# Transfers of the preparation begun by ScalarE, rows kept six tiles ahead, state stored at every second piece

## Chip, cores and metric

The kernel runs on one core of one Trainium2 chip. The metric is the device time of one execution in microseconds (us), the median of several runs.

## What is computed

The reference takes x of 2 × 2048 tokens with 256 features and does two sublayers, each with a LayerNorm before it and one after it, and a residual. The first is attention with one head of 128 and rotary positions. The second is a mixture of experts that is run twice over the same state z:

```python
for _ in range(LOOPS):                       # LOOPS = 2
    z_norm = _rmsnorm(z, norm_w)
    logits = z_norm @ router_w               # 8 experts
    scores = softmax(logits)
    topk_vals, topk_idx = top_k(scores, 2)   # then normalised to sum 1
    mixed = 0
    for e in range(8):
        mixed += cw[:, e] * _swiglu(z_norm, w1[e], w3[e], w2[e])
    z = z + mixed                            # silu(x @ w1) * (x @ w3) @ w2, F = 512
```

The result is x1 + LayerNorm(z), where x1 is what the attention sublayer left.

## The kernel before

Everything is float32. The first 427 us are the attention, with its normalisation, projections and output; the weights of the experts are loaded to SBUF beside it and stay there. The change doesn't touch that part. The rest, about 850 us, is the mixture of experts, and it is one loop over 142 tiles: 71 for each pass over z. A tile is 128 rows, each row a (token, expert) pair; all rows of a tile belong to one expert. Rows that two groups of tokens bring are tiled apart: group 0 holds 18 of the 32 blocks of 128 tokens, group 1 holds 14, so that the routing of one group can be worked out while the tiles of the other are computed.

**One tile, from row to row.** GpSimd gathers the 128 rows of z from DRAM by an indirect transfer (xg<-zd, L948, `gather`). SyncE writes the rows of two tiles at once to DRAM in order (xs<-xg, L961, `keep`) and reads them back in four strided transfers (xb<-xs, L970, `load`), so that VectorE can turn them into 128-column blocks (xT<-xb, L257, `turned`). TensorE multiplies with w1 and w3 (p<-wall,xT, L993, `hidden`), ScalarE takes Silu (a<-p, L1002), VectorE multiplies the halves (g<-a,p, L1007, `gate`). The hidden rows go the same way: SyncE stores them in DRAM (gd<-g, L1012), reads two tiles back in four transfers (gb<-gd, L1019, `hidden_back`), VectorE turns them (gT<-gb, L257, `turn_hidden`), TensorE multiplies with w2 (py<-wall,gT, L1035, `mix`). ScalarE scales the rows (y<-py,rms, L1048, `give`), and GpSimd scatters them by an indirect transfer into a buffer in DRAM (given<-y,to, L1049) that holds both experts' rows of a token side by side.

**The order.** The kernel is a Python program that writes instructions in the order in which each engine will run them. `slot(m, ...)` (L1550) writes one step of the tile loop. It does, in this order: `hidden_back` of tiles m−3 and m−2 if m is odd, `gate` of m−1, `turn_hidden` of m−4, `give` of m−6, `fetch_rows(m)`, `turned` of m+2, then half of the preparation work, `hidden` of m, `mix` of m−5, and the other half of the preparation. In `fetch_rows` a pair's xb is loaded up to AHEAD = 4 tiles ahead, its xs is written up to AHEAD + 1 = 5 tiles ahead, and rows are gathered up to GATHER = 7 tiles ahead. Below, P(m) is the start of hidden(m) on TensorE.

**The preparation.** `advance` (L1543) takes pieces from a generator between the steps of the tile loop, each with a cost, until a credit for half a slot is used up (mostly SLOT/2 = 8). `plan` (L1574) says which generator runs from which slot on:

- from slot 0: the routing of group 1 for the first pass (`b0.before`);
- from slot 21: `a1.fetch(0, 24)` loads z of group 0 from DRAM (9 transfers z<-zd, L291), when the routing for pass two approaches;
- from about slot 42: `a1.before`. It first runs `logits`: for each block of two tiles load the rows that were given (given<-given, L308, 528 KB, two blocks ahead), multiply by the gains on ScalarE and add on VectorE (`add_first`, L329), add the second expert's rows on GpSimd (`add_second`), take the sum of squares on ScalarE. Then `route` and `lists` work out which token goes where, and at each of their first 9 pieces `store(i)` (L433) stores one block of z to DRAM (zd<-z, 264 KB), from where the tiles of pass two gather;
- from slots 68 and 78 on: the same for group 1 (`b1.fetch`, `b1.before`), 7 blocks;
- from slot 100 on: `a1.fetch(1)` loads z of group 0 again for the end; then `a1.finish` adds what pass two gave and does the last LayerNorm and the residual (given loads, x<-x1d L788, out<-z L783/L787), and `b1.ready` loads z and x1 of group 1 ahead;
- after the loop: `b1.last` finishes group 1.

All these direct transfers, those of the tile loop and those of the preparation, are begun by SyncE before the change, but for four of `last`. GpSimd begins the indirect ones.

Of the kernel before, what the change touches and what calls it, by code (L numbers as in the profile page):

```python
# [29 lines left out]
def attn_moe_kernel(  # L30
# [16 lines left out]
    nc = tc.nc  # L47

    ctx.enter_context(tc.manual_schedule())
    B, S, D = x.shape  # L50
# [29 lines left out]
    ob = out.rearrange("b s d -> (b s) d").rearrange("(n t p) d -> n p t d", t=2, p=P)  # L80
# [10 lines left out]
    x1d = [  # L91
        dram.tile([P, 2, D], F32, name=f"x1d{i}", tag=f"x1d{i}") for i in range(T // 2)
    ]
# [169 lines left out]

    SLOT, HALF = 16, 8
    STEP = 4
    sent = [[] for _ in range(LOOPS)]

    class Turn:
# [18 lines left out]
        def load(self):  # L287

            i = self.loaded
            if 2 * i < self.n:  # L290
                nc.sync.dma_start(  # L291
                    out=self.z[:, 2 * i : 2 * i + 2, :D],
                    in_=zrows(self.of_loop, self.t0 // 2 + i)[:, :, :D],
                )
                self.loaded += 1
# [89 lines left out]
        def logits(self):  # L385

            n = self.n
            last = self.loop - 1
            nc.vector.tensor_copy(self.z[:, :, D:Z], raw[:, self.ts, :])
            y = {i: self.load_given(last, i, nc.sync) for i in range(2)}  # L390
            yield SLOT
            ms = rpool.tile([P, NM], F32, tag="fl_sd", name="ms")[:, :n]
            rms = rpool.tile([P, NM], F32, tag="fl_sh", name="rms")[:, :n]
            lg = self.lg.rearrange("p e t -> p t e")
            done, part = 0, None

            for i in range(n // 2 + 4):
                if i + 2 < n // 2:
                    y[i + 2] = self.load_given(last, i + 2, nc.sync)
                if part is not None:  # L400
                    w = part.stop - part.start
                    nc.vector.tensor_tensor(
                        lg[:, part, :],
                        self.z[:, part, D:Z],
                        rms[:, part].rearrange("p (t o) -> p t o", o=1).to_broadcast([P, w, E]),
                        ALU.mult,
                    )

                    nc.vector.tensor_copy(self.z[:, part, D], rms[:, part])
                    part = None  # L410
                if 0 <= i - 3 < n // 2 and ((i - 3) % 3 == 2 or i - 3 == n // 2 - 1):
                    part = slice(done, 2 * (i - 2))
                    done = part.stop
                    w = part.stop - part.start
                    nc.vector.tensor_scalar(
                        ms[:, part], rms[:, part], 1.0 / D, RMS_EPS, ALU.mult, ALU.add
                    )
                    nc.gpsimd.tensor_tensor(rms[:, part], ms[:, part], neg_half[:, :w], ALU.pow)
                if 0 <= i - 2 < n // 2:
                    for t in range(2 * i - 4, 2 * i - 2):  # L420
                        sq = rpool.tile([P, D], F32, tag="sq", name="sq")
                        nc.scalar.activation(
                            sq, self.z[:, t, :D], AF.Square, accum_out=rms[:, t : t + 1]
                        )
                if 0 <= i - 1 < n // 2:
                    self.add_second(i - 1, y.pop(i - 1))
                if i < n // 2:
                    self.add_first(last, i, y[i])
                yield 10 if i < n // 2 else 6
            assert part is None and not y  # L430

        def store(self, i):
            nc.sync.dma_start(  # L433
                out=zrows(self.loop, self.t0 // 2 + i), in_=self.z[:, 2 * i : 2 * i + 2, :R]
            )

# [193 lines left out]
        def lists(self, pool, tag, keep):  # L630
# [12 lines left out]
            for h in range(parts + (3 if keep else 2)):  # L643
# [3 lines left out]
                if 0 <= i < parts:  # L647
# [12 lines left out]
                    if not keep:  # L660
                        yield STEP
                        if i == 0:
# [89 lines left out]
        def before(self, pool, tag, keep=True):  # L752
            self.lg = rpool.tile([P, E, NM], F32, tag="lg", name="lg")[:, :, : self.n]
            if self.loop == 0:
                yield from self.first_logits()
            else:
                yield from self.logits()

            for i, cost in enumerate(
                itertools.chain(self.route(pool, tag), self.lists(pool, tag, keep))  # L760
            ):
                if self.loop > 0 and i < self.n // 2:
                    self.store(i)
                yield cost

        def out_(self, i, z, x1, pool=False):

            mv, rstd = ln_stats(z, 2)
            yield
            nb = ln_bias(mv, rstd, 2)  # L770
            to = self.z[:, 2 * i : 2 * i + 2, :D]
            for t in range(2):
                nc.scalar.activation(
                    to[:, t, :],
                    z[:, t, :],
                    AF.Identity,
                    bias=nb[:, t : t + 1],
                    scale=rstd[:, t : t + 1],
                )
            yield  # L780
            (nc.gpsimd if pool else nc.vector).tensor_tensor(to, to, x1, ALU.add)
            yield
            nc.sync.dma_start(out=ob[self.t0 // 2 + i], in_=to)  # L783

        def load_x1(self, i, x1=None):
            if x1 is None:
                x1 = fp.tile([P, 2, D], F32, tag="x1", name="x1", bufs=3)  # L787
            nc.sync.dma_start(out=x1, in_=x1d[self.t0 // 2 + i])  # L788
            return x1

        def fetch(self, loop, cost):
# [6 lines left out]
        def finish(self):  # L798

            n = self.n // 2  # L800
            y, x1, ends = {}, {}, []
            for h in range(2 * n + 9):
                for end in list(ends):
                    if next(end, True):
                        ends.remove(end)
                i, odd = divmod(h - 7, 2)
                if not odd and 0 <= i < n:
                    ends.append(self.out_(i, self.z[:, 2 * i : 2 * i + 2, :D], x1.pop(i)))
                    next(ends[-1])
                i, odd = divmod(h - 5, 2)  # L810
                if not odd and 0 <= i < n:
                    self.add_second(i, y.pop(i))
                    x1[i] = self.load_x1(i)
                i, odd = divmod(h - 4, 2)
                if not odd and 0 <= i < n:
                    self.add_first(self.loop, i, y[i])
                i, odd = divmod(h, 2)
                if not odd and i < n:
                    y[i] = self.load_given(self.loop, i, nc.sync)
                yield 7  # L820
            assert not ends

# [34 lines left out]
        def last(self):  # L857


            n = self.n // 2  # L860
            sums, y = [], []
# [30 lines left out]
                    second = y[i][t][:, 1, :]  # L892
                    nc.scalar.mul(second, second, self.gain(self.loop, i, 1, t))

            ends = [self.out_(i, sums[i], self.x1[i], i % 2 == 1) for i in range(n)]
            weigh(0)
            weigh(1)
            for i in range(n + 3):
# [21 lines left out]

    A = ND * F
    AHEAD = 4
    GATHER = 7
    TURN = 2
    BACK = 4
    LAG = 5
# [137 lines left out]
    NJ = len(jobs)  # L1064
# [10 lines left out]
    def fetch_rows(m, rest=()):  # L1075


        nonlocal gathered, kept, loaded

        def load():  # L1080
            nonlocal loaded
            if loaded < kept:
                one, other = pair(loaded)
                one.load(other)
                loaded += 1 if other is None else 2

        def keep():
            nonlocal kept
            one, other = pair(kept)
            n = 1 if other is None else 2  # L1090
            if gathered >= kept + n:
                one.keep(other)
                kept += n

        def gather():
            nonlocal gathered
            held = sum(jobs[i].i % 2 == 0 for i in range(loaded, gathered))
            if jobs[gathered].turn.to is not None and (jobs[gathered].i % 2 or held < 2):
                jobs[gathered].gather()
                gathered += 1  # L1100

        if loaded <= min(m + AHEAD, NJ - 1):
            load()
        if kept <= min(m + AHEAD + 1, NJ - 1):
            keep()
        for _ in range(2):
            if gathered <= min(m + GATHER, NJ - 1):
                gather()
        if loaded <= min(m + TURN + 1, NJ - 1):
            while jobs[loaded].turn.to is None or jobs[min(loaded + 1, NJ - 1)].turn.to is None:  # L1110
                next(rest)
            while loaded <= min(m + TURN + 1, NJ - 1):
                gather()
                keep()
                load()
# [531 lines left out]
```

## Time and profile before

| what | value |
|---|---|
| median of 3 runs | 1275.72 us (1273.36 to 1276.16) |
| the profiled execution | 1276.36 us |
| its span, first to last instruction | 1274.6 us |
| mean granted TensorE clock in it | 0.978 |
| TensorE matmul busy | 1168.7 us (92%) |
| VectorE busy | 673.5 us (53%) |
| GpSimd busy | 519.6 us (41%) |
| ScalarE busy | 424.4 us (33%) |
| transfers on SyncE's queue (q1) | 181.85 MB, 53.5% of the 16 DMA engines' span |
| transfers on GpSimd's queue (q0) | 37.61 MB, 10.6% |
| transfers on ScalarE's queue (q10) | 3.16 MB, 0.7% |

The profile names an operation by the program's names, what it writes and what it reads (`xb<-xs`), with the line. PE is TensorE's matmul, DVE is VectorE, ACT is ScalarE, POOL is GpSimd, SP is SyncE. "SPq" is SyncE's queue: issuing a transfer isn't counted as busy, but takes the queue's time, and a line "SPq L970 <- DMA xs<-xg" is time in which it stood before a transfer of L970 until xs had landed. The chain that ended last has TensorE for 27%, transfers for 23% (xs<-xg alone 9%), issue for 16%, SyncE's queue for 13% and VectorE for 11%. In the page's row of DMA shares the tile loop has 0.6 to 0.9 of the 16 DMA engines busy in most slices, so landings depend on what else is under way.

The stages of the tile loop, from the start of hidden(0) at 427.3 us, are, with what runs beside: to about 528 the routing of group 1; to 690 the first pass, from about 550 on with the loads of z; to 800 `a1.before`; to 850 the loads for group 1; to 956 `b1.before`; to 1131 the second pass with its loads for the end; to 1215 `a1.finish` and `b1.ready`; then the last tiles and `b1.last`.

### The profile page before, as it was taken

To read this page: it belongs to the slowest core of one execution; us is meant where nothing else is said; L and a number is where in the kernel's file an instruction comes from. 1 tells how busy PE (TensorE), PEld (TensorE's weight loads), DVE (VectorE), ACT (ScalarE), POOL (GpSimd) and SP (SyncE) were. 2 spreads that over 40 slices of the span, in tenths; PEclk is the share of its full clock that TensorE was granted. 3 is DMA by queue.
4 is the path that set the end of the run, shared out by engine and by line. 5 is a ranking of instruction groups with operands and counts; after the bars stand their busy time and mean duration, and the time that the engine had idled before them with its cause. 6 is when DMAs were issued, how large, how long until landed. Compare 5 with 4: busy or idle time off the path is not lost.

```text
span 1274.6 us, 16856 instructions
## 1 busy us (share of the span) xinstructions
PE 1168.7 (92%) x4230; PEld 719.6 (56%) x4230; DVE 673.5 (53%) x1809; ACT 424.4 (33%) x945; POOL 519.6 (41%) x870
## 2 busy tenths in 40 slices
PE   6989999999989799999999886999899999998895
PEld 3546777766666355555555444555455555554563
DVE  4646676767895457332331676334683333367224
ACT  3444343445645221221221631224312222234124
POOL 3541434341123433443442752445534444466523
PEclk9999999999999899999999987999899999999998
DMA  4124465611112577777767896899967798899955
GB/s 133 50 44 97 116 155 119 157 51 33 43 34 69 151 201 202 205 210 215 209 197 222 267 215 165 217 245 272 242 189 207 216 249 216 239 274 282 259 170 181
DMA packets 273099, 223.69 MB, mean 175 GB/s; under 512 B 112240, under 2 KB 226288, under 8 KB 273008
## 3 DMA queue, kind: packets, MB, share of 16 engines
q1 hardware_dynamic: 256640, 181.85, 53.5%
q0 software_dynamic: 13632, 37.61, 10.6%
q10 hardware_dynamic: 2736, 3.16, 0.7%
q8 instruction: 40, 0.66, 0.2%
q14 instruction: 51, 0.42, 0.1%
HBM read 130.90 MB, written 91.62 MB: 175 GB/s over the span
## 4 chain that ended last, share of the span: by engine, by line
PE 27%; DMA 23%; issue 16%; SPq 13%; DVE 11%; POOL 7%; ACT 2%; DVEq 0%; ACTq 0%; POOLq 0%
DMA xs<-xg 9%; PE sc L1357 7%; PE po L1404 6%; SPq L970 6%; PE p L993 5%; SPq L1019 5%; DMA gd<-g 4%; DMA gb<-gd 4%; PE tp_p L1391 4%; POOL xg L948 3%; PE py L1035 3%; DMA given<-given 2%; DMA xg<-zd,token 1%; PE py L1441 1%; POOL given L1049 1%
## 5 line engine op out<-in xcount | busy, mean ns | idle before, releaser
L993 PE MATMUL p<-wall,xT 128*128 x1136 | 521.2, 603 | 14.8 <-DVE xT L257 8.3
L993 PEld LDWEIGHTS p<-wall,xT 128*128 128x128 f32 x1136 | 218.1, 194 | 237.0 <-issue 223.8
L1035 PE MATMUL py<-wall,gT 128*128 x1136 | 275.3, 386 | 23.6 <-DVE gT L257 22.8
L1035 PEld LDWEIGHTS py<-wall,gT 128*128 128x128 f32 x1136 | 215.6, 191 | 120.5 <-issue 76.4
L1049 POOL DMA_INDIRECT given<-y,to x142 | 141.7, 998 | 346.9 <-ACT y L1048 321.3
L1007 DVE TENSOR_TENSOR g<-a,p 128x512 f32<-128x512 f32 x142 | 96.7, 681 | 196.4 <-issue 155.3
L257 DVE STREAM_TRANSPOSE gT<-gb 128x512 f32<-128x512 f32 x142 | 100.0, 705 | 177.8 <-DMA gb<-gd 177.8
L948 POOL DMA_INDIRECT xg<-zd,token x142 | 141.7, 998 | 89.5 <-DMA xs<-xg 66.9
L1048 ACT ACTIVATE y<-py,rms 128x264 f32<-128x264 f32 (+1 forms) x142 | 67.4, 474 | 322.2 <-PE py L1035 313.8
L1002 ACT ACTIVATE a<-p,rms 128x512 f32<-128x512 f32 x142 | 97.2, 685 | 189.8 <-PE p L993 145.7
L1357 PE MATMUL sc<-qkT 128*128 128x512 f32 x256 | 130.9, 597 | 2.0 <-ACT pr L1376 1.2
L1404 PE MATMUL po<-pt,v 128*128 128x256 f32 x512 | 127.3, 382 | 0.4 <-ACT y L1444 0.4
L1404 PEld LDWEIGHTS po<-pt,v 128*128 128x128 f32 x512 | 97.2, 191 | 51.8 <-issue 40.5
L1376 ACT ACTIVATE pr<-sc,nm 128x512 f32<-128x512 f32 x128 | 88.5, 694 | 89.1 <-DVE nm L1368 89.1
L1364 DVE TENSOR_REDUCE m<-sc 128x1 f32<-128x512 f32 x128 | 87.6, 686 | 45.4 <-PE sc L1357 44.2
L1391 PE MATMUL tp_p<-ident,pr 128*128 128x128 f32 x512 | 80.4, 276 | 10.6 <-ACT pr L1376 9.7
L1391 PEld LDWEIGHTS tp_p<-ident,pr 128*128 128x128 f32 x512 | 63.7, 143 | 40.4 <-ACT pr L1376 14.7
L185 POOL TENSOR_TENSOR rds<-rs_v,neg_half 128x2 f32<-128x2 f32 (+1 forms) x24 | 20.4, 849 | 153.7 <-DVE rs_v L184 153.1
L1395 ACT COPY pt<-tp_p 128x512 f32<-128x512 f32 x88 | 51.4, 584 | 62.2 <-PE tp_p L1391 61.4
L257 DVE STREAM_TRANSPOSE xT<-xb 128x256 f32<-128x256 f32 x142 | 57.1, 404 | 6.4 <-DMA zd<-y 4.6
L236 POOL TENSOR_SCALAR wall<-wall,nwp 128x1024 f32<-128x1024 f32 x16 | 45.6, 2850 | 10.8 <-DMA wall<-in_L_ffn_w 10.8
L1214 PE MATMUL pm<-wqkvT,hT 128*128 128x392 f32 x128 | 46.3, 505 | 0.0
(249 smaller groups left out, 978.4 us busy)
## 6 DMA issues: line engine op xcount, KB each, us to landing
gd<-g SPq DMA_DIRECT2D x142, 256.0 KB
gb<-gd SPq DMA_DIRECT2D x284, 128.0 KB
xs<-xg SPq DMA_DIRECT2D x70, 257.0 KB
xb<-xs SPq DMA_DIRECT2D x280, 64.0 KB
wall<-in_L_ffn_w SPq DMA_DIRECT2D x96, 128.0 KB
given<-given SPq DMA_DIRECT2D x16, 528.0 KB
z<-zd SPq DMA_DIRECT2D x32, 256.0 KB
given<-given SPq DMA_DIRECT2D x11, 512.0 KB
```

The lines of the kernel that those rows point to most:

```text
L257: nc.vector.transpose(out=dst.rearrange("p c (a t) -> p a c t", t=32), in_=src.rearrange("p (a c d) -> p a c d", a=4, c=n),)
L948: i = nc.gpsimd.indirect_dma_start(out=self.xg[:, k, :], out_offset=None, in_=zd[self.loop][: (SPLIT if self.i < WHOLE else T) * P, :], in ...
L993: nc.tensor.matmul(ps, lhsT=self.xT[:, c, :], rhs=wall[:, bass.ds(self.e, 1), o : o + F].rearrange("p o f -> p (o f)"), start=(c == 0), st ...
L1002: nc.scalar.activation(self.a, p1, AF.Silu, scale=self.rms)
L1007: nc.vector.tensor_tensor(g, self.a, self.p3, ALU.mult)
L1035: nc.tensor.matmul(py[:, :w], lhsT=self.gT[:, f, :], rhs=wall[:, bass.ds(self.e, 1), o : o + w].rearrange("p o d -> p (o d)"), start=(f == 0),
L1049: i = nc.gpsimd.indirect_dma_start(out=given[self.loop], out_offset=bass.IndirectOffsetOnAxis(ap=self.row(self.turn.to), axis=0), in_=y, i ...
L1357: nc.tensor.matmul(sc[u], lhsT=qkT[b][:, 0, qi * P : (qi + 1) * P], rhs=qkT[b][:, 1, c * KC : (c + 1) * KC], start=True, stop=True,)
L1364: nc.vector.tensor_reduce(nms[t][:, c : c + 1], sc[u], AX.X, ALU.max)
L1376: nc.scalar.activation(prs[u], sc.pop(u), AF.Exp, bias=nms[t], scale=SCALE, accum_out=s4s[t][:, c : c + 1],)
L1391: nc.tensor.transpose(tp[:, j, i, :], pr[:, k : k + P], ident)
L1404: nc.tensor.matmul(pos[p], lhsT=vn[p * QG // NT][:, 2 * g + j, :HD], rhs=pt[:, j, :], start=(g == 0 and j == 0), stop=(g == NS - 1 and j = ...
```

## The change

Five edits come together. A name `bulk` stands for ScalarE's queue, and the preparation's transfers are begun by it: the loads of z, of given (in `logits` and `finish`), of x1, the stores of z, and the stores of the result in `finish` (`last` keeps SyncE's). That is about 100 transfers. `logits` yields HALF once before its first loads. `store` comes at every second piece of `route` and `lists` instead of each. xs is written up to KEEP = 6 tiles ahead instead of 5 (AHEAD itself stays 4). Rows are gathered up to 8 tiles ahead instead of 7.

```diff
     SLOT, HALF = 16, 8
     STEP = 4
+
+    bulk = nc.scalar
...
-                nc.sync.dma_start(
+                bulk.dma_start(
                     out=self.z[:, 2 * i : 2 * i + 2, :D],
                     in_=zrows(self.of_loop, self.t0 // 2 + i)[:, :, :D],
...
-            y = {i: self.load_given(last, i, nc.sync) for i in range(2)}
+            yield HALF
+            y = {i: self.load_given(last, i, bulk) for i in range(2)}
             yield SLOT
...
-                    y[i + 2] = self.load_given(last, i + 2, nc.sync)
+                    y[i + 2] = self.load_given(last, i + 2, bulk)
...
         def store(self, i):
-            nc.sync.dma_start(
+            bulk.dma_start(
                 out=zrows(self.loop, self.t0 // 2 + i), in_=self.z[:, 2 * i : 2 * i + 2, :R]
...
-                if self.loop > 0 and i < self.n // 2:
-                    self.store(i)
+                j, odd = divmod(i, 2)
+                if self.loop > 0 and not odd and j < self.n // 2:
+                    self.store(j)
                 yield cost
...
-            nc.sync.dma_start(out=ob[self.t0 // 2 + i], in_=to)
+            engine.dma_start(out=ob[self.t0 // 2 + i], in_=to)
...
-            nc.sync.dma_start(out=x1, in_=x1d[self.t0 // 2 + i])
+            bulk.dma_start(out=x1, in_=x1d[self.t0 // 2 + i])
...
-                    y[i] = self.load_given(self.loop, i, nc.sync)
+                    y[i] = self.load_given(self.loop, i, bulk)
...
     AHEAD = 4
-    GATHER = 7
+    KEEP = 6
+    GATHER = 8
...
-        if kept <= min(m + AHEAD + 1, NJ - 1):
+        if kept <= min(m + KEEP, NJ - 1):
             keep()
```

More of the change, by code (lines that the diff above doesn't have):

```diff
@@ L761, in before, with out_ @@
             ):
-                if self.loop > 0 and i < self.n // 2:
-                    self.store(i)
+                j, odd = divmod(i, 2)
+                if self.loop > 0 and not odd and j < self.n // 2:
+                    self.store(j)
                 yield cost
-        def out_(self, i, z, x1, pool=False):
+        def out_(self, i, z, x1, engine, pool=False):
             mv, rstd = ln_stats(z, 2)
@@ L807, in finish @@
                 if not odd and 0 <= i < n:
-                    ends.append(self.out_(i, self.z[:, 2 * i : 2 * i + 2, :D], x1.pop(i)))
+                    ends.append(self.out_(i, self.z[:, 2 * i : 2 * i + 2, :D], x1.pop(i), bulk))
                     next(ends[-1])
@@ L893, in weigh @@
                     nc.scalar.mul(second, second, self.gain(self.loop, i, 1, t))
-            ends = [self.out_(i, sums[i], self.x1[i], i % 2 == 1) for i in range(n)]
+            ends = [self.out_(i, sums[i], self.x1[i], nc.sync, i % 2 == 1) for i in range(n)]
             weigh(0)
```

## The prediction

> **What bounds the kernel now.** I read the shares first, then TensorE by stage, then SyncE's waits, then timelines. TensorE is busy 1168.7 of 1274.6 us, but that is an average. The windows view for the first expert matmul alone (line L993, 8 records a tile; columns: window, length, matmul busy and records, weight loads, clock, DMA share, GB/s) shows where it isn't the limit:
>
> ```profile
> 427.30:528.00 100.70, 73.59 (x160) 30.63 (x160) 0.98 0.68 190
> 528.00:690.00 162.00, 107.91 (x241) 45.81 (x242) 1.00 0.75 208
> 690.00:800.00 110.00, 57.59 (x119) 23.66 (x119) 0.89 0.84 218
> 800.00:850.00 50.00, 33.83 (x76) 14.25 (x75) 1.00 0.92 235
> 850.00:956.00 106.00, 67.38 (x144) 27.72 (x143) 0.97 0.87 234
> 956.00:1131.00 175.00, 122.27 (x272) 51.48 (x271) 1.00 0.85 228
> 1131.00:1215.00 84.00, 48.24 (x105) 20.31 (x106) 0.98 0.96 271
> ```
>
> Where TensorE never waits a tile takes 5.21 us in the first loop (3.43 for L993, 1.78 for L1035) and 5.16 in the second. Records/8 times that, against the length: 956–1131 is full (34 tiles, 175.4 of 175). 690–800 loses 110−14.9×5.21 = 32.5 us, 850–956 loses 106−18×5.16 = 13.1, 1131–1215 loses 84−13.1×5.16 = 16.3, 528–690 about 5, and tiles 12 to 19 of the first window 3.6 by their starts. That is 70 us, and all the change can win. Who is late there? SyncE's own waits (us in total, times, longest):
>
> ```profile
> SPq L970 <- DMA xs<-xg: 103.3, 33, 5.7
> SPq L1012 <- DVE g L1007: 71.0, 39, 7.0
> SPq L1019 <- DMA gd<-g: 40.5, 24, 4.6
> SPq L970 <- DMA z<-zd: 1.6, 3, 0.7
> SPq L970 <- DMA given<-given: 1.5, 2, 1.1
> SPq L970 <- DMA zd<-z: 1.3, 2, 1.0
> ```
>
> SyncE begins every transfer of the tile loop in program order and stands at each wait with all later ones behind it. The last three lines matter more than their size: xb (L970) uses nothing of z, given or zd. In the kernel as built, SyncE and ScalarE draw all transfers' completion counters from one set of eight, in program order, and a transfer waits until its counter's previous user has landed.
>
> How an in-order SyncE costs time, in the timelines of ScalarE, SyncE and TensorE at the start of 690–800:
>
> ```profile
> 686.68 0.69 ACT L1002 ACTIVATE a<-p,rms 128x512 f32<-128x512 f32 x1 [1.24 <-PE p L993]
> 701.50 0.92 ACT L329 ACTIVATE given<-given,gains 128x264 f32<-128x264 f32 x2 [14.13 <-DMA given<-given]
> ```
> ```profile
> 683.62 0.43 SPq L1012 DMA_DIRECT2D gd<-g  x1
> 688.44 2.94 SPq L970 DMA_DIRECT2D xb<-xs  x4
> ...
> 694.52 1.48 SPq L308 DMA_DIRECT2D given<-given  x3
> ```
> ```profile
> 703.85 3.52 PE L1035 MATMUL py<-wall,gT 128*128 x8 [5.06 <-DVE gT L257]
> ```
>
> SyncE stood 4.8 us for xs, began given only at 694.5, given took 7.0 us to 701.5, and ScalarE stood at its multiplication for 14.13 us with y and Silu of the tile loop behind it. The start of hidden(52) came 11.97 us after hidden(51)'s, 6.8 too late. Later steps of this stage: 57→58 12.54, 60→61 16.25, 61→62 8.24.
>
> **The change part by part.** *Moving about 100 transfers from SyncE to ScalarE.* Each costs SyncE 0.5–0.6 us (z 0.60, zd 0.57, given 0.5), so some 55 us of SyncE work leave, and ScalarE gets them at 0.39–0.59 each (its few own). ScalarE is busy 35.3 of 110 us in 690–800, and its idle time ahead of y (322 us in all) hides most; without that cover each is half a microsecond ahead of a Silu. Ten loads and nine stores there, a third exposed and waiting a little for counters themselves: I take 4 us, bounds 0 and 10.
>
> The Trainium skill (page "DMA: Bandwidth & Descriptors", section "Issuing engines are not separate DMA queues") speaks against the part: starting transfers on several engines only saves the sequencer's issue time, since all run on the same DMA engines. By that rule the gain is at most the exposed part of 55 us, near nothing, because landings don't get shorter (DMA share 0.84–0.96). The rows say that the loss is order, not issue time: the 8 us by which given began late and the 6.8 us after it. I take the rows: that stall goes. But the same order turns round:
>
> *The counters now tie two engines together.* In the changed kernel as built, some 80 SyncE transfers wait for a ScalarE transfer to land, many for one that ScalarE begins one or two tiles later. Before, both stood in SyncE's own order, and the earlier had mostly landed. Price: ScalarE begins a bulk transfer 0.6 us (after y) or 4.8 us (after Silu) after the start P(n) of hidden(n) in its tile; it is released at R, that plus the landing. Landings (issue to landing, medians of the trace): z 4.5, given 6.9, zd 5.7–7.6, x1 6.2. Where xb of tile A waits, the rest of xb (1.2), xs (0.4), gd's landing, three gb issues (1.4), gb's landing and the transposition (0.7) follow, due 3.5 us into tile A+4 for its mix: P(A+4) ≥ R + gd + gb + 0.2. Where xs waits, R − 1.0 + gd + gb. Free is 10.3 to 10.4 us from P(A+2) to P(A+4). gd lands in 3.1–3.3 in quiet stretches, 5.8–6.3 in crowded ones, gb in 4.0 and 4.8. Stage by stage:
>
> 956–1131 (z for the last finish, tiles 101–109): xb of 101, 103, 105, 107 wait for the z load two tiles on. R = P(A+2)+0.6+4.5 = 5.1; 5.1+3.3+4.0+0.2 = 12.6 against 10.3: +2.3 a pair, four pairs, and gb of 101 +1.3: **+10.5**, in a stage that loses nothing now. 800–850 (z of the second group): the same for 69 and 71: **+4**.
>
> 850–956: xs of 75 waits for given of 77's second half: 4.8+6.9−1.0+3.9+4.4 = 19.0, +8.7; xs of 77 for given of 79: 0.6+6.9+7.3 = 14.8, +4.5; xs of 85 for zd of 87: 13.6, +3.3; small ones 0.4. That is 17, and I leave 3 of the old 13.1: **+7**.
>
> 690–800: the stalls of 51/52 and most of the three that followed go, 3 of 32.5 stay. New: gb of 49 waits for given of 50: its gT is there at 5.2+0.6+7.0+1.4+4.0+0.7 = 18.9 after P(49), due at 13.9: +5; xb of 50 and 52 +1 each; gd of 59 behind zd of 59's second half +3; ScalarE 4. 14+3 = 17 left of 32.5: **−15**.
>
> 1131–1215: xb of 121, 131, 133 and xs of 135 wait for x1 or z two tiles on, 14.9 each by quiet landings, 17–18 by crowded ones: 16 to 29 us in all against 16.3 now; I take 22: **+6**.
>
> *Rows six ahead, gathers eight.* As built, xs stands one tile earlier in SyncE's order, so xb finds it landed. In 528–690 SyncE's round is xs landing 5.0 + issues 5.6 = 10.6 a pair against TensorE's 10.42; the wait goes, and so do the 5 us there, and about 2 in tiles 12–19. z loads of tiles 22–32 give 3.5 back by ties one tile long: **−1** and **−2**.
>
> *Stores at every second piece, HALF before the first given.* Nine stores of 264 KB now begin one piece apart; the chain of waits has them in this stage, at 742–766:
>
> ```profile
> 744.29 6.65 DMA gb<-gd
> 751.00 9.51 DMA zd<-z
> 760.57 0.55 SPq L433
> ```
>
> Spacing them takes crowding from gd and gb (medians 5.8 and 5 there, 3.1 and 4.0 quiet); counted in the −15. The last store comes nine pieces later, and gathers wait for it and for the lists, still unfinished then: 0, at most +5. HALF moves one start by half a tile: 0.
>
> Sum: −2 −1 −15 +4 +7 +10.5 +6 = +9.5. The profiled execution took 1276.4 us (span 1274.6), 0.6 above the median 1275.7: 1285.9 on its scale, **1285** on the median's.
>
> **The rivals.** *A, the forecast (0.46)*: ties cost about what their sums say, the stage that was full loses 10, 690–800 wins 15: 1278 to 1300.
> *B, faster (0.26)*: SyncE reaches the tied transfers late anyway. A tie is free if released before P(A+2)+2.8 (10.3−7.5); z would have to land 2.2 us after its start rather than 4.5, or SyncE's program would have to run a tile ahead now that its own 55 us and its 103.3 us of xs waits are gone, so that tied transfers have a tile's slack. Then 690–800 wins 22, 850–956 and 1131–1215 8 each, the early stages 4: 1276−42 = 1234; with half of the ties paid, 1250. For it: the xs wait is the largest in SyncE's list. Against it: the sums already spend the slack that there is (in 956–1131 gd begins 4.4 us after its hidden, the mix comes 29.3 after).
> *C, much slower (0.20)*: ScalarE's transfers wait in turn for counters of SyncE's tied ones, and Silu and y stand behind them, as behind given at 687–701. With the long landings of the trace (given 9.9, zd 10.8, gd 7.8–10.5) the same sums give +36: 1312.
> *D, no change (0.08)*: wins and ties cancel, 1276.
>
> **How the numbers follow.** What a measurement of this kernel can tell from no change is about 0.2%, 2.6 us. B gives faster 0.26, D same 0.08, A and C slower 0.66. The range leaves out the far ends of B and C: 1248 to 1308. A's own is 1278 to 1300.
>
> **What would show it.** Right: records of L993 in a 956–1131-like stretch pace at over 5.4 us a tile for tiles 101–110; SyncE's waits at L970 and L1012 ended by z, given, zd, x1 grow from 1–2 us to tens; the xs line falls from 103 to under 40; ScalarE's 14 us stop ahead of L329 is gone. Wrong: tiles 101–110 still at 5.16 (B), or ScalarE's queue waiting ahead of its transfers for over 1 us at many places (C). If gd and gb land in 3–4 us in 690–800, B's −22 there holds even with ties.

## The result, and the profile after

The changed kernel is slower: 1317.95 us median (1315.82 to 1321.79), against 1274.54 us for the kernel before, run beside it. The ratio is 1.035 with a 95% interval of 1.031 to 1.039. The forecast was 1285 us and its range ended at 1308. The profiled execution has a span of 1318.0 us, 43.4 more than before.

Below, the loss of a stage is counted by tiles, not by fixed times, since the stages shift: the time from the start of hidden of its first tile to that of its end tile, less 5.21 us (first pass) or 5.16 us (second) a tile. "Beside" names the preparation that runs there.

| tiles | beside | before, us | after, us | difference | forecast |
|---|---|---|---|---|---|
| 12–20 | routing of group 1, first pass | 3.6 | 1.4 | −2.2 | −2 |
| 20–50 | z loads | 4.5 | 0.1 | −4.4 | −1 |
| 50–66 | a1.before | 34.1 | 25.5 | −8.6 | −15 |
| 66–74 | z loads of group 1 | 0.2 | 0.7 | +0.5 | +4 |
| 74–92 | b1.before | 13.9 | 32.4 | +18.5 | +7 |
| 92–118 | z loads for the end | 0.0 | 10.2 | +10.2 | +10.5 |
| 118–136 | a1.finish, b1.ready | 14.3 | 38.8 | +24.5 | +6 |

The rest is 4.5 us behind the start of the last hidden (54.2 after 49.7), about 1 at the start and −0.8 in tiles 136–141. The sum is 43.4 but for rounding.

SyncE's waits in the kernel after (us in total, times, longest), in answer to those of before:

```profile
SPq L1024 <- DMA gd<-g: 119.9, 39, 5.1
SPq L1017 <- DVE g L1012: 78.2, 30, 7.4
SPq L975 <- DMA given<-given: 32.7, 7, 8.4
SPq L1024 <- DMA z<-zd: 21.1, 5, 10.1
SPq L975 <- DMA z<-zd: 18.7, 8, 5.4
SPq L975 <- DMA xs<-xg: 10.7, 5, 2.9
```

The 103.3 us for xs are 10.7, as the row edit promised. In their place SyncE stands for transfers that xb (L975) and gb (L1024) use nothing of. All its waits for given, z, zd, x1 and out come to 127 us, against 10.9 before. The traces show the link: SyncE's and ScalarE's transfers report their landing on the same eight semaphores, GpSimd's on eight others. The wait for gd's landing ahead of gb has tripled (40.5 before), but that is no sign of loss: in e1 and e2 below, which are faster than the kernel before, it is 115.0 and 122.5 us.

In the stage that was full, the timelines of SyncE and ScalarE show one such tie:

```profile
1044.48 0.42 SPq L1017 DMA_DIRECT2D gd<-g  x1
1044.95 5.36 SPq L975 DMA_DIRECT2D xb<-xs  x4
1050.42 0.54 SPq L966 DMA_DIRECT2D xs<-xg  x1
```
```profile
1045.84 0.47 ACT L1053 ACTIVATE y<-py,rms 128x256 f32<-128x256 f32 x1 [2.75 <-PE py L1040]
1045.84 0.53 ACTq L293 DMA_DIRECT2D z<-zd  x1
```

Four xb issues take 2.6 us when nothing holds them, and 5.36 here: the third waited until 1049.09 for the z load that ScalarE began at 1045.84 and that landed at 1049.08. In tiles 100–112 the stage lost 10.1 us where 10.5 was forecast, and SyncE stood 9.7 us for z loads there. The sum agrees better than its parts: the forecast had 2.3 us at each of four pairs of tiles, and the trace has 6.6 us at one step (105 to 106) and 0.5 to 1.9 at three others.

Around 1149 us, in tiles 118–136, the same views show what the price list did not have:

```profile
1149.02 0.60 ACT L777 ACTIVATE z<-z,ln_nb,ln_rstd 128x256 f32<-128x256 f32 x1 [12.00 <-DVE ln_nb L206]
1149.08 0.53 ACTq L310 DMA_DIRECT2D given<-given  x1
1149.52 0.59 ACT L777 ACTIVATE z<-z,ln_nb,ln_rstd 128x256 f32<-128x256 f32 x1
1149.65 0.73 ACTq L792 DMA_DIRECT2D x<-x1d  x1
```
```profile
1118.41 10.86 SPq L975 DMA_DIRECT2D xb<-xs  x4
...
1135.46 1.80 SPq L1024 DMA_DIRECT2D gb<-gd  x4
...
1145.56 1.80 SPq L1024 DMA_DIRECT2D gb<-gd  x4
1147.40 0.45 SPq L1017 DMA_DIRECT2D gd<-g  x1
1148.07 8.69 SPq L975 DMA_DIRECT2D xb<-xs  x4
1157.17 0.34 SPq L966 DMA_DIRECT2D xs<-xg  x1
```

In the second of these views SyncE, at 1118.41, issued one xb and then stood 8.4 us until a given load that ScalarE had begun at 1117.66 had landed (1127.38). VectorE then stood 4.1 us for these xb and later 4.2 us for the gb that SyncE began at 1135.46. ScalarE stood 12.00 us for the bias of a LayerNorm (ln_nb) that VectorE had not got to; for 2.2 us of it VectorE stood for GpSimd. Behind ScalarE's wait lay given and x1, and SyncE's last two xb issues came at 1155.49 and 1156.13, the latter as x1, begun at 1149.65, landed (1156.12). So a tie had its part in making late the engine that begins the transfers of the next ties: a ring through engines that all work in order. The prediction let ScalarE begin a transfer 0.6 or 4.8 us after P(n); here it was later by the length of ScalarE's own wait.

### The profile page after: what moved, and what is told of

Its sections match the earlier page's. It is cut to its first block, busy times and chain, and to the rows that moved or that the text cites. A ratio compares the mean times of both kernels' runs of the same rounds, so it can differ in the third digit from the quotient of the medians.

```text
span 1318.0 us, 16792 instructions
## 1 busy us (share of the span) xinstructions
PE 1183.7 (90%) x4230; PEld 728.8 (55%) x4230; DVE 672.7 (51%) x1809; ACT 424.9 (32%) x945; POOL 521.2 (40%) x870
## 4 chain that ended last, share of the span: by engine, by line
PE 49%; DMA 16%; DVE 12%; issue 10%; POOL 7%; SPq 3%; ACT 2%; ACTq 0%; POOLq 0%; DVEq 0%
PE p L998 20%; PE py L1040 10%; PE sc L1362 6%; PE po L1409 5%; PE tp_p L1396 3%; DMA gd<-g 3%; DMA gb<-gd 3%; DMA given<-given 3%; POOL xg L953 2%; POOL given L1054 2%; DMA xs<-xg 2%; SPq L975 2%; PE py L1446 1%; DMA z<-zd 1%; DVE m L1369 1%
## 5 line engine op out<-in xcount | busy, mean ns | idle before, releaser
L998 PE MATMUL p<-wall,xT 128*128 x1136 | 525.0, 606 | 13.9 <-DMA xb<-xs 8.7
L998 PEld LDWEIGHTS p<-wall,xT 128*128 128x128 f32 x1136 | 220.3, 196 | 238.3 <-issue 224.3
L1040 PE MATMUL py<-wall,gT 128*128 x1136 | 283.9, 395 | 51.2 <-DVE gT L257 36.9
L1040 PEld LDWEIGHTS py<-wall,gT 128*128 128x128 f32 x1136 | 220.6, 196 | 151.3 <-issue 104.5
L236 POOL TENSOR_SCALAR wall<-wall,nwp 128x1024 f32<-128x1024 f32 x16 | 45.6, 2852 | 10.9 <-DMA wall<-in_L_ffn_w 10.9
L1362 PEld LDWEIGHTS sc<-qkT 128*128 128x128 f32 x256 | 41.9, 193 | 9.1 <-issue 3.4
```

The costliest lines, as they stand in the source:

```text
L998: nc.tensor.matmul(ps, lhsT=self.xT[:, c, :], rhs=wall[:, bass.ds(self.e, 1), o : o + F].rearrange("p o f -> p (o f)"), start=(c == 0), st ...
L1040: nc.tensor.matmul(py[:, :w], lhsT=self.gT[:, f, :], rhs=wall[:, bass.ds(self.e, 1), o : o + w].rearrange("p o d -> p (o d)"), start=(f == 0),
L1362: nc.tensor.matmul(sc[u], lhsT=qkT[b][:, 0, qi * P : (qi + 1) * P], rhs=qkT[b][:, 1, c * KC : (c + 1) * KC], start=True, stop=True,)
```

## The experiments

Theory T is the forecast's: the loss is the tie of SyncE's transfers to ScalarE's through counters that both draw from one set. Its rivals were that the row edit or the later stores hurt, that two queues crowd the DMA engines, and that ScalarE's own order holds its transfers. Ratios are to the kernel before, run beside each. There the kernel before took 1287 to 1290 us, not the 1274.5 of the main result, and there is no trace of it from there. So ratios are the measure of what an edit costs; losses by tiles, which come from one trace each, can be compared with those of the kernel before or the changed one only with a doubt of up to 12 to 16 us in all. Traces of different runs whose code is the same up to tile 66 differ by up to 3 us in 50–66.

### The parts alone

**e1**: the row edit alone.

```diff
-    GATHER = 7
+    KEEP = 6
+    GATHER = 8
...
-        if kept <= min(m + AHEAD + 1, NJ - 1):
+        if kept <= min(m + KEEP, NJ - 1):
```

> Only the row edit: xs written up to six tiles ahead and rows gathered up to eight ahead; all direct transfers stay on SyncE, stores at every piece. Theory T (the loss of the whole change is the tie of SyncE's transfers to ScalarE's through shared completion counters): this part is a gain by itself, the 4.4 us of tiles 20-50 and about 2 of tiles 12-20 go, some of the 34, 14 and 14 us of the three preparation stages too: 1262 to 1270 us. Rival R1 (deeper rows crowd the DMA engines, so gd and gb land later): 1276 to 1290.

Measured: 0.991 (0.988 to 0.994). Right in size, and it disposes of R1 for the whole kernel. But the stages surprised: 12–50 lose 1.5 instead of 8.1 and 50–66 lose 24.7 instead of 34.1, while 74–92 lose 20.1 (13.9 before) and 118–136 lose 19.2 (14.3). The row edit pays in the first pass. That it costs 11 us in the second isn't shown: as much could be the difference of 12 us between the two measurements of the kernel before.

**e2**: the change with its queue edit undone.

```diff
-    bulk = nc.scalar
+    bulk = nc.sync
```

> The changed kernel with bulk = SyncE, so that only the row edit, the stores at every second piece and the HALF before the first loads remain. Theory T: no ties to another queue, tiles 100-112 lose 0 again, 74-92 and 118-136 lose 10 to 14 each as before: 1258 to 1270. Rival R1 or a rival in which the later stores delay the gathers: 1290 or more.

Measured: 0.987 (0.983 to 0.991); the whole change takes 4.8% longer than this (1.0348/0.9872, each from its own pair of runs). The queue edit is all of the loss and more. 100–112 lose 0. But 74–92 lose 22.7 and 118–136 lose 20.0, and 50–66 still lose 18.2. Large stalls are left in these stages, although SyncE hardly stands for xs.

**e3**: the queue edit alone; rows and stores as before.

> The kernel before with only the queue edit: the preparation's transfers begun by ScalarE, rows five and seven ahead, stores at every piece. Theory T: all of the loss is here, and the row edit's gain is missing: 1315 to 1335, tiles 100-112 lose about 10, 118-136 over 30. Rival R1: near 1276, within 8.

Measured: 1.038 (1.035 to 1.042), as expected in sum. By stage 50–66 lose 38.1, 74–92 25.7, 118–136 28.8 (over 30 was expected) and 100–112 only 5.2, half of what was expected. Tiles 20–50 lose 10.8. The row and store edits win 1.3% by themselves (e2), but with the queue edit hardly anything (1.035 after 1.038, intervals overlapping).

### Is it the counters?

**e4**: all transfers stay on the queues of the change. An added wait is meant only to move them in the order in which counters are given out.

```diff
-    bulk = nc.scalar
+    class Bulk:
+        last = None
+        def dma_start(self, **kw):
+            i = nc.scalar.dma_start(**kw)
+            if self.last is not None:
+                tc.add_manual_dep(i.ins, self.last.ins.name, ...)
+            return i
+    bulk = Bulk()
...
-            nc.sync.dma_start(out=gd[:P] if self.second is not None else gd[P:], in_=g)
+            bulk.last = nc.sync.dma_start(out=gd[:P] if self.second is not None else gd[P:], in_=g)
```

> The changed kernel, all transfers on the same queues as there, but each ScalarE transfer of the preparation also waits until the last gd store written before it has landed. That wait falls between y and Silu, mostly into idle time of ScalarE; what it changes is the order in which counters are handed out: SyncE's transfers then wait only for ScalarE transfers of one or two tiles back, never for later ones. Theory T: tiles 100-112 lose 0 instead of 10, 74-92 10 to 14 instead of 32, 118-136 10 to 16 instead of 39: 1240 to 1262. Rival R2 (two queues at once crowd the DMA engines, or ScalarE's transfers are late behind its own waiting instructions whatever the counters do): the same transfers are begun at nearly the same times, so 1305 to 1325.

Measured: 1.026 (1.022 to 1.029). The expectation failed in sum, and the time lies where R2 put it. 100–112 lose 0.0, as T says, but 118–136 lose 39.1, 74–92 lose 27.2 (10 to 14 was expected) and 50–66 lose 33.6. ScalarE's waits in this kernel tell why:

```profile
ACT a L1024 <- DMA gd<-g: 94.7, 19, 11.4
```

L1024 is Silu here. The wait that I had taken to lie in idle time held it for 94.7 us. So e4 alone decides nothing but 100–112.

**e5**: the same with the gd store one older, to wait for a landing that is mostly past.

```diff
-            if self.last is not None:
+            if len(self.stores) >= 2:
...
-                    self.last.ins.name,
+                    self.stores[-2].ins.name,
```

> As e4_order, but each ScalarE transfer waits for the gd store one older than there, which has landed about 3 us before in a healthy round, so ScalarE should not stand for it. SyncE's transfers then wait for ScalarE transfers of the same tile at latest, none of a later one. Theory T (ties to later transfers cost; what e4 lost was its added wait, 95 us of Silu standing for gd): Silu's wait for gd under 20 us, tiles 100-112 lose 0, 74-92 under 25, 118-136 under 25: 1255 to 1285 scaled to a before of 1276. Rival R3 (ScalarE's own order: its transfers stand behind waiting instructions, and Silu behind them, whatever the counters do): 118-136 still over 35 and 1300 or more.

Measured: 1.000 (0.998 to 1.002). Silu's wait for gd is down from 94.7 to 9.0 us. 100–112 lose 0.0, 74–92 lose 19.3 (32.4 in the change), 118–136 lose 26.6 (38.8; under 25 was expected). The same transfers on the same two queues, with the direction of the ties turned, are back at the time of the kernel before: the 3.5% are gone. The last 1.3% to e2 are not, in 50–66 (25.1, e2 18.2) and 118–136; in 50–66 turning the ties changed nothing (25.5 in the change). R3 expected 1300 or more and is out as the main cause. SyncE still stands 92 us for the preparation's transfers in e5 (127 in the change). What fell most is the time that it stood for transfers that ScalarE began only after SyncE had come to stand: from 53 us in nine waits to 20 in three. For those begun earlier it stood 71 us in the change and 69 in e5. How long it stands says less than for what.

**e6**: only the z loads on ScalarE; **e12**: the same loads on GpSimd, whose transfers have counters of their own. All else as e2. The edit from e6 to e12:

```diff
-                nc.scalar.dma_start(
+                nc.gpsimd.dma_start(
                     out=self.z[:, 2 * i : 2 * i + 2, :D],
```

> The changed kernel with only the z loads on ScalarE, all other transfers of the preparation on SyncE (e2_sync plus 32 transfers). Theory T: the stages with z loads get their ties back: tiles 100-112 lose 10 instead of 0, 66-74 about 1, 118-136 two ties of b1.ready, 0 to 4 more than e2's 20: e2 + 10 to 15. Rival R3: ScalarE waits for nothing in tiles 100-112, so they lose 0: e2 + 0 to 3.

> As e6_zonly, but the 32 z loads are begun by GpSimd, whose transfers take their counters from another set: no transfer of the tile loop on SyncE waits for a z load. Theory T: tiles 100-112 lose 0 (e6: 13.6), 66-74 under 1 (e6: 7.3), unless GpSimd's own work of issuing a load, ahead of a gather or scatter, adds something (0 to 4 us in all); the rest as e2: ratio to before 0.985 to 0.992. Rival R2 (a second queue crowds the DMA engines whatever its counters): 100-112 lose 5 or more, ratio 1.000 or more.

Measured: e6 1.005 (1.003 to 1.007), e12 0.985 (0.982 to 0.987). The first matmul's windows over tiles 100–112, e6 and then e12:

```profile
997.00:1072.50 75.50, 44.76 (x96) 19.23 (x96) 0.91 0.63 181
```
```profile
984.00:1045.90 61.90, 43.16 (x96) 18.24 (x96) 1.00 0.85 232
```

The same 12 tiles and the same loads take 75.5 us with the loads on ScalarE and 61.9, which is no loss, on GpSimd. In e6 the DMA engines are less busy (0.63 against 0.85), so they are not what is short. SyncE's waits for z in the window of e6 are

```profile
SPq L975 <- DMA z<-zd: 8.8, 3, 3.4
SPq L1024 <- DMA z<-zd: 2.8, 1, 2.8
SPq L1017 <- DMA z<-zd: 1.9, 1, 1.9
```

together 13.5 us, against the 13.6 that the stage loses; e12 has none there. A second queue costs nothing by itself here; R2 is out for this stage, though it may have a part in the 1.3% that e5 keeps over e2. e12 changes the engine along with the counters, but e4 and e5 kept both engines and lost 0.0 here too: theory T is shown for this stage. e6 cost more than expected (1.8% over e2, 23 us): 66–74 lose 7.3 instead of about 1 and 74–92 lose 28.8. In e12 one stage is not as in e2: 118–136, which has z loads of its own, loses 9.3 instead of 20.0, but tiles 136–141 lose 8.0 instead of 1.0. Why was not tried.

### Which transfers cost where

**e7**: only given in `logits` and the z stores on ScalarE. **e8**: only given, x1 and out of the last finish. All else as e2.

> The changed kernel with only the loads of given in logits and the stores of z on ScalarE, the rest on SyncE. Tells where the loss of tiles 74-92 comes from. Theory T: the ties of 75 to 87 are all here: 74-92 lose about 32 as in the changed kernel (e2: 23), 50-66 about 25 (e2: 18), other stages as e2: e2 + 15 to 18. Rival R4 (those stages lost by what z loads before them leave late): e2 + 0 to 5.

> The changed kernel with only the transfers of the last finish and of x1 (given, x1, out) on ScalarE, the rest on SyncE. Theory T with ScalarE's order: x1 and given stand behind ScalarE's LayerNorm instructions, which wait for VectorE, which waits for gb and xb, which wait on SyncE for x1: 118-136 lose 35 to 40 (e2: 20), other stages as e2: e2 + 15 to 20. Rival R2 (crowding by many transfers at once): 118-136 under 25, e2 + 0 to 5.

Measured: e7 1.002 (1.000 to 1.004), e8 0.999 (0.997 to 1.002), 1.5% and 1.2% over e2, 19 and 16 us. e7 has its loss in 74–92 (29.9, e2 22.7) and more than expected in 50–66 (31.0, e2 18.2). e8 has it in 118–136 (33.1, e2 20.0), a little under the expected 35 to 40. The ring is there too: ScalarE's longest stand for ln_nb at the last LayerNorm (L777) is 11.0 us in e8 and 5.3 in e2. With e6 the three parts add up to 4.6% over e2, and the whole change is 4.8% over it: in sum the parts hardly act on each other, as far as e2's interval of ±0.4% can tell.

### What the old stalls are

**e9**: e2 without the z stores, so that the second pass reads the old state; the update of z between the passes is left out. **e10**: e2 without the loads of given and the additions in `logits`.

```diff
-                if self.loop > 0 and not odd and j < self.n // 2:
-                    self.store(j)
...
-                    in_=zrows(self.of_loop, self.t0 // 2 + i)[:, :, :D],
+                    in_=zrows(0, self.t0 // 2 + i)[:, :, :D],
...
-                in_=zd[self.loop][: (SPLIT if self.i < WHOLE else T) * P, :],
+                in_=zd[0][: (SPLIT if self.i < WHOLE else T) * P, :],
```

> e2_sync without the 16 stores of z after the first pass (the second pass gathers from, and the end loads, the old state: the update of z between the passes is left out of what they read). Tells what the stalls are that stayed in e2 (18 us in tiles 50-66, 23 in 74-92) although SyncE no longer stands for xs. Theory U: the routing's own chain (squares, the power on GpSimd, scores, lists, one after another on in-order engines with g, gT and xT behind them) makes them, so without the stores they stay within 4 us each; 118-136 keeps its 20: e2 - 0 to 8. Rival V (the stores crowd the DMA engines, so gd and gb land late): 50-66 under 10, 74-92 under 15: e2 - 15 to 20.

> e2_sync without the loads of given in logits and without the additions that use them (the experts' outputs of the first pass aren't added before the second routing). Theory U: the stalls at 58-61 and 86-90 lie behind the loads, in the routing, and stay; only 81-83 (about 8 us, VectorE waiting for given) goes: e2 - 6 to 12. Rival W (the 528 KB loads and their waits make the stalls): 50-66 under 8 and 74-92 under 10: e2 - 20 to 25.

Measured: e9 0.978 (0.974 to 0.981), e10 0.973 (0.968 to 0.977). Without the stores 50–66 lose 11.3 (e2 18.2) and 74–92 lose 19.7 (22.7). Without given, 11.7 and 6.6. So of the 22.7 in 74–92, 16 hang on given, more than U expected; in 50–66 stores and given are some 7 each, with a doubt of about 3. Against e2's ratio that is 12 and 19 us won: U expected at most 8 and 12, V and W at least 15 and 20, so neither U nor the two rivals has it alone. What the last 5 us of 50–66 hang on was not tried, and neither was what makes the 20 us of 118–136, which both runs leave as they are (20.0 and 19.4). In e2, VectorE's longest wait in 836 to 950 us is for given:

```profile
DVE z L332 <- DMA given<-given: 16.1, 3, 6.2
```

### A version that takes what paid

**e11**: all on SyncE, rows six and eight ahead in the first pass only, spaced stores for the first group only.

```diff
-                j, odd = divmod(i, 2)
+                j, odd = divmod(i, 2) if self.g == 0 else (i, 0)
...
-        if kept <= min(m + KEEP, NJ - 1):
+        if kept <= min(m + (KEEP if m < NX else AHEAD + 1), NJ - 1):
...
-            if gathered <= min(m + GATHER, NJ - 1):
+            if gathered <= min(m + (GATHER if m < NX else 7), NJ - 1):
```

> A version that takes from each edit what paid: all on SyncE; rows six and eight ahead in the first pass only, five and seven in the second; stores at every second piece for the first group only; the HALF stays. If the row edit costs in the second pass what e1's stages show (74-92 +6, 118-136 +5): 74-92 lose 14, 118-136 14, 50-66 18: ratio to before 0.979 to 0.984, faster than e2. Rival: those stages are as long because they are reached earlier with the same amount of work: no better than e2's 0.987.

Measured: 0.979 (0.976 to 0.982), the fastest that computes the whole result, faster than both kernels and than e2. 74–92 lose 18.6 and 118–136 lose 16.8, where 14 each was expected: 7 us less than e2, by undoing the row edit in the second pass and, in 74–92, the spacing of the stores; the run doesn't part the two. 50–66, with the same code as e2, also lose 2.8 us less, so the stages are less sure than the ratio.

## Why the prediction was wrong, step by step

**The ties: right in direction and in mechanism.** Slower, by ties of SyncE's transfers to ScalarE's through shared counters. The Trainium skill ("DMA: Bandwidth & Descriptors", section "Anatomy of one DMA — SWDGE (gpsimd) path") says of the DMA engines in general that any semaphore wait of a transfer happens on the issuing sequencer; SyncE's 5.36 us for four xb, with every later transfer behind them, agree.

**The price of the ties: too high in sum.** With ScalarE's own 4 us the forecast's terms come to 71. The ratios of the whole change and e2 put the queue edit at 4.8%, 61 us. By tiles, the change less e2, it is 7.3 in 50–66 (forecast 10, and 4 for ScalarE), 0.5 in 66–74 (4), 9.7 in 74–92 (17), 10.1 in 100–112 (10.5), 18.8 in 118–136 (22), and nothing of the 3.5 in 20–50. So "The counters now tie two engines together" was not priced too low, and the ring at 1149 us did not make its stage dearer than the tie sum. That 100–112 came out to half a microsecond is luck: the same stage lost 5.2 us in e3 and 13.6 in e6, and none of the three has the even steps of the forecast.

**The failed step: "3 of 32.5 stay", "I leave 3 of the old 13.1", and the 16 us of 1131–1215 taken as replaced by ties.** The forecast took the old stalls of the preparation's stages as the work of SyncE's order, to vanish with it. Without the ties its terms win 62 us (29.5, 10.1 and 16.3 in the three stages, 6.5 in tiles 12–50). e2, which is the change without the queue edit and in which SyncE stands for almost no xs, wins 1.3%, 16 us (11 to 22). That is 46 us short; less the 10 by which the ties were overpriced, it is the difference between the forecast +9.5 and the measured +43.4, to within 2 us. By tiles e2 still loses 18.2, 22.7 and 20.0 us in the three stages, 61 where the forecast kept 6; as its trace is from a slower measurement, up to 12 of that may not be the edit's. What the stalls hang on is shown in part: on given and the stores in 50–66 and on given in 74–92 (e9, e10). In 118–136 the cause stays open.

Why did I read it so? The one stall that I followed, at tile 51, was of that kind: e1 and e2 don't have it, with given still on SyncE, so it went with the row edit and needed no second queue. I let it stand for the others. Those at 57–61 and 85–90 are still in e2, most of them a tile later. The reading itself was loose too: in the lines shown SyncE's stand for xs is 4.4 us, not 4.8, and most of the time from 688.44 to 694.52 was the issue of other transfers. The chain of waits that I quoted for 742–766 shows gb and zd landing, and e9 shows that the stores do cost, but the transfers and the chain of given, additions and routing remain whoever begins them. For the wins that is nearer to the rule of the Trainium skill that I set aside ("DMA: Bandwidth & Descriptors", section "Issuing engines are not separate DMA queues": only issue time is saved): moving the preparation's transfers to ScalarE with the ties turned (e5) has 74–92 at 19.3 against 22.7, but 50–66 at 25.1 against 18.2, and a time no better than the kernel before. By the rule alone the change would have been near nothing; the loss of the ties isn't in it.

**ScalarE's stand for given** did go: 28.8 us before L329, 2.6 after. It wasn't the limit: e2 has 26.9 us of it and is the faster by 4.8%.

**The row edit** won its 7 us in tiles 12–50 (6.6), and the 3.5 us of ties there were not paid. Whether it costs in 74–92 and 118–136, which the forecast didn't consider, is open (e1, e11).

**Stores at every second piece, HALF.** Counted inside the −15. e2 against e1, run side by side: 6.5 us won in 50–66, 2.6 lost in 74–92, the latter no more than traces differ.

**The rivals.** B needed tied transfers to be late anyway; its test (tiles 101–110 at 5.16) failed. C came within 6 us of the time, but by another way, which is luck: it priced the ties by long landings, and they cost less than the middle estimate. Of its mechanism, ScalarE standing ahead of its own transfers, three Silus that waited 18 us in all for zd, xs and z are seen. D is out.

## What to carry to other kernels

Before a transfer is moved to another engine's queue, look at which completion counters it shares and with whom: an engine can come to wait for a transfer that another engine begins only later, and that wait is in nobody's code. A queue with counters of its own (here GpSimd's) took the same loads without loss in the stage that had been full. And one stall that has been followed to its cause is evidence for that stall, not for the stage; a kernel with the suspected wait alone removed would have shown what remains, and here that kernel (e2) won 16 us of the 62 that were forecast.

## What the runs showed of the hardware

TensorE can pay twice for a stall. In e2 it idled 5.00 us after the last matmul of a mix, and the next tile, 59, then ran slower: its hidden (L998) took 5.09 us, that of tile 60 took 3.60.

```profile
738.40 0.85 PE L490 MATMUL pc<-ch,before 128*128 128x144 f32 x2 [5.00 <-issue]
739.52 5.09 PE L998 MATMUL p<-wall,xT 128*128 x8
746.23 3.60 PE L998 MATMUL p<-wall,xT 128*128 x8
```

The window over the slow tile (busy time of five engines, then granted clock, DMA share, GB/s) shows the clock:

```profile
738.40:744.60 6.20, 6.20 (x13) 3.37 (x14) 5.75 (x27) 0.69 (x1) 0.43 (x2) 0.68 0.89 235
```

A shorter stall can do it, and a longer one need not. In e6 TensorE idled 2.23 us ahead of tile 84 (first two views: the hidden and the window of its first 3.4 us); in the changed kernel it idled 3.13 us ahead of a mix, and the tile behind it took 3.67 us (last view):

```profile
899.20 5.40 PE L998 MATMUL p<-wall,xT 128*128 x8 [2.23 <-ACT a L1007]
```
```profile
899.20:902.60 3.40, 3.40 (x4) 1.43 (x5) 1.73 (x4) 3.32 (x12) 2.39 (x5) 0.52 0.83 235
```
```profile
899.15 1.97 PE L1040 MATMUL py<-wall,gT 128*128 x8 [3.13 <-ACT sq L425]
901.03 3.67 PE L998 MATMUL p<-wall,xT 128*128 x8
```

The Trainium skill ("TensorE: Matmul & The Clock Gate", Part 1) has the clock halve after an idle window of about 3.4 us. The halving is here (0.52 over 3.4 us), but it came after 2.23 us of idle time, less than that window; the measurement stands. In the two cases shown, the stall cost 1.5 and 1.8 us beyond its own length, which the losses by tiles contain and which a sum of waits does not.
